# A two-step graph layer with nucleus attention on one core: ACT copies results out of PSUM, the kept weights' sum comes from the mask pass, queries are projected at the head of a slot

## The chip, the cores and the metric

The kernel runs on one NeuronCore of a Trainium2 chip. Its engines are PE (matrix products, into PSUM), DVE (vector operations), ACT (functions of one operand with scale and bias), POOL (a second, slower vector engine, here for columns of one number per row) and SP (which only issues transfers here). Each takes its own instructions in order and waits on semaphores for the others. The metric is the time of one execution on the device in microseconds; less is better.

## The reference

The input x is 3327x256, adj (S) 3327x3327 with few entries off zero. All is float32. The layer does two steps of diffusion and of attention, and a layer norm at the end:

```python
R = S + jnp.eye(N, dtype=X.dtype)
R = R / R.sum(-1, keepdims=True)
Z = jnp.zeros_like(X)
Xf = X
Xa = X
for n in range(STEPS):                               # 2 steps
    A = _top_p_attention(Xa, W1, W2, W3)
    Xf = R @ Xf
    Xa = A @ Xa
    Z = Z + Xf @ U1[n].T + Xa @ U2[n].T
h = X + Z                                            # then (h - mean) / sqrt(var + eps) * g + b
```

and `_top_p_attention` is a softmax of which each row keeps only its largest entries, until their sum reaches 0.9, scaled to sum 1 again:

```python
q = X @ W1.T @ W2.T
k = X @ W3.T
probs = jax.nn.softmax(q @ k.T / TAU, axis=-1)
idx = jnp.argsort(-probs, axis=-1)
sp = jnp.take_along_axis(probs, idx, axis=-1)
cs = jnp.cumsum(sp, axis=-1)
keep_sorted = cs - sp < TOP_P
mask = jnp.zeros(probs.shape, dtype=bool).at[rows, idx].set(keep_sorted)
A = probs * mask
return A / jnp.maximum(A.sum(-1, keepdims=True), 1e-12)
```

The X of this is `h = max(layernorm(x), 0)` of the input x, and the output is x plus what the layer returns.

## The kernel before

Rows are cut into 26 tiles of 128. A step goes through the tiles in slots: the loop at the end of `guess_graph_layer` (L719 to L750) has in slot i four tiles in different stages of work.

- `settle(i)` on DVE decides which weights of tile i are kept. L585 is a pass over the 128x3328 weights `e` that keeps in `w` those under a guessed cut, with their sum; 20 MAX8 (L589) and 5 or 6 rounds (L594, L596) find the largest of what is left; L605, the mask pass, sets to zero in `e` what is not kept. POOL gives the wanted sum (`need`, L586).
- `first(i + 1)` and in step 1 `second(i + 1)` guess the cut of the next tile. `first` makes two passes over `e` on ACT (L520) and then a chain on POOL of one-column operations (L524 to L542). `second` makes one more pass on DVE (`jv`, L549) and a longer POOL chain (L551 to L574). The column that they end with is what L585 waits for.
- `spread(i + 1)` gives the 26 matmuls of diffusion (`diffuse`, L662), which come out of a generator and are put between others; each needs a piece of adj, which SP loads five blocks of 128x128 at a time (`AD`, `at`, three buffers).
- `attend(i - 1)` multiplies the kept weights by Xa: 26 transposes of `e` (`pt`, L637), each four copied out of PSUM by ACT (`eT`, L639), 26 matmuls into `pa` (L647). Column 256 of the right side is 1, so column 256 of `pa` is the sum of the kept weights. DVE takes its reciprocal (L651), ACT scales by it (L652).
- `weights(i + 2)` projects the queries of the tile after (PE, `pq`, L455 and L457; ACT copies `qT`; DVE takes from PSUM what a first guess needs, L462 to L465), makes the logits (PE, `pl`, L476) and their exps (ACT, L480 to L484), and sums and guesses on POOL (L489 to L511).
- Then what is left of diffusion, and in step 0 `prep(1, ...)`, which makes keys and queries of step 1 from the tile, in step 1 `finish`, which multiplies by U1 and U2 (`pz`), adds X (DVE, L684, out of PSUM), norms, adds x and writes the rows out (SP, L693).

A scheduler puts every engine's instructions in one order before the program runs, from the order of the code and its own estimates. What an engine does at a given moment is fixed by that order alone: an instruction whose semaphore has not come holds back all that stand behind it. PSUM holds two buffers each of `pl` and `pt` (which `pq`, `pk` and `pg` share), and one each of `pa` (which `pz` shares) and `pr`.

`search_graph_layer` is another, slower way to the same result, taken only where a guess has failed; it doesn't run in these executions.

## Time and profile before

| | |
|---|---|
| time, median of 3 runs | 2558.28 us (2556.28 to 2563.46) |
| the profiled execution | 2557.2 us |
| its span in the trace | 2555.4 us |
| mean granted clock of PE in it | 0.877 |
| busy: PE, weight load, DVE, ACT, POOL | 1945.5 (76%), 1524.5 (60%), 1100.5 (43%), 866.6 (34%), 900.7 (35%) us |
| moved by DMA | 102.24 MB, 40 GB/s over the span |

The span is the time from the first to the last instruction that the trace shows; 1.8 us of the execution's own time lie around it. Times below count from the span's start. In a row, L585 is line 585 of the kernel; `w<-e,g` are the tiles that it writes and reads. A number in brackets at a row's end is the time in which the engine stood idle before it, with the instruction whose end released it. Two rows that follow each other may overlap by up to 0.2 us, since an instruction begins while the one ahead of it still writes. A row may stand for several equal instructions in succession (x8). PE does a float32 matmul in two passes, which count as two, and a transpose in one.

### The profile page before, as it was taken

Reading aid. Unit: us, or ns where it says so; the run is one execution under the profiler, and the core shown is the slowest. Engines: PE = TensorE matmul, PEld = TensorE weight load, DVE = VectorE, ACT = ScalarE, POOL = GpSimd, SP = SyncE. Lnnn points to the kernel's source line nnn. Section 1 sums busy time; section 2 is a strip of 40 time slices with the busy share of each in tenths; the row PEclk is TensorE's granted clock in tenths of the full one; section 3 lists DMA queues with packets and bytes.
Section 4 is the critical chain, followed back from the end, with each engine's and each line's share of the span. In section 5 each row is a group of like instructions: output and inputs, shape, how many; then the busy total and the mean of one; then the engine's idle time right before and its main releaser. Section 6 shows DMA issues by size and latency. Waiting matters only on the chain.

```text
span 2555.4 us, 26919 instructions
## 1 busy us (share of the span) xinstructions
PE 1945.5 (76%) x9055; PEld 1524.5 (60%) x9055; DVE 1100.5 (43%) x2969; ACT 866.6 (34%) x1588; POOL 900.7 (35%) x2541
## 2 busy tenths in 40 slices
PE   6957887888888887887777767777667776777767
PEld 5735665766666675775556645566455664556645
DVE  2155543535354443531754454344543445434451
ACT  4344344343434334234232223322233222332221
POOL 4153222232322222214534433344333443334431
PEclk9978888999999998988888887888878888888888
DMA  4210011111111111111111111111111111111100
GB/s 133 69 29 27 13 32 43 39 48 33 48 44 39 48 39 43 39 39 31 49 32 45 37 32 37 36 46 38 31 34 39 46 38 31 40 34 45 38 26 12
DMA packets 58597, 102.24 MB, mean 40 GB/s; under 512 B 7250, under 2 KB 25169, under 8 KB 58449
## 3 DMA queue, kind: packets, MB, share of 16 engines
q1 hardware_dynamic: 55936, 98.85, 13.3%
q10 hardware_dynamic: 2512, 1.57, 0.2%
q8 instruction: 73, 1.20, 0.2%
q14 instruction: 76, 0.61, 0.1%
HBM read 96.99 MB, written 3.41 MB: 39 GB/s over the span
## 4 chain that ended last, share of the span: by engine, by line
DVE 33%; POOL 29%; PE 14%; ACT 13%; issue 9%; DMA 0%; ACTq 0%; POOLq 0%; DVEq 0%
DVE cand L589 9%; DVE w L585 7%; ACT ja L520 7%; DVE e L605 7%; PE pl L476 4%; ACT e L480 4%; POOL g L564 4%; DVE cand L596 3%; DVE bb L594 3%; PE pz L681 3%; PE pa L647 2%; PE pr L662 2%; POOL g L503 1%; POOL g L499 1%; POOL g L507 1%
## 5 line engine op out<-in xcount | busy, mean ns | idle before, releaser
L476 PE MATMUL pl<-k,qT 64*128 64x512 f32 (+1 forms) x832 | 226.0, 672 | 357.4 <-ACT e L480 321.8
L639 ACT COPY eT<-pt 128x512 f32<-128x512 f32 (+1 forms) x364 | 197.7, 556 | 706.8 <-PE pt L637 704.1
L520 ACT ACTIVATE ja<-e,g 128x3328 uint8<-128x3328 f32 x104 | 319.3, 3070 | 237.5 <-POOL g L503 237.4
L476 PEld LDWEIGHTS pl<-k,qT 64*128 64x128 f32 x832 | 87.8, 232 | 494.1 <-ACT e L480 400.8
L662 PE MATMUL pr<-xf,at 128*128 128x256 f32 x1352 | 368.9, 409 | 16.8 <-ACT xf L671 15.6
L585 DVE SCALAR_TENSOR_TENSOR w<-e,g 128x3328 f32<-128x3328 f32 x52 | 192.0, 3693 | 438.0 <-POOL g L574 225.2
L662 PE MATMUL pr<-x,at 128*128 128x257 f32 x1352 | 371.7, 417 | 0.3 <-DMA at<-in_adj 0.2
L647 PE MATMUL pa<-x,eT 128*128 128x257 f32 x1352 | 326.6, 386 | 10.6 <-ACT eT L639 10.6
L647 PE MATMUL pa<-xa,eT 128*128 128x257 f32 x1352 | 319.5, 380 | 0.5 <-ACT eT L639 0.5
L662 PEld LDWEIGHTS pr<-x,at 128*128 128x128 f32 x1352 | 267.9, 211 | 46.1 <-issue 4.2
L662 PEld LDWEIGHTS pr<-xf,at 128*128 128x128 f32 x1352 | 253.7, 203 | 59.5 <-ACT xf L671 20.1
L647 PEld LDWEIGHTS pa<-x,eT 128*128 128x128 f32 x1352 | 254.8, 193 | 46.9 <-ACT eT L639 11.9
L647 PEld LDWEIGHTS pa<-xa,eT 128*128 128x128 f32 x1352 | 255.1, 190 | 37.3 <-ACT eT L639 1.2
L589 DVE MAX8 cand<-w 128x8 f32<-128x168 f32 (+1 forms) x1040 | 249.2, 317 | 1.6
L637 PE MATMUL pt<-ident,e 128*128 128x128 f32 x1352 | 227.5, 301 | 4.7 <-DVE e L605 4.7
L637 PEld LDWEIGHTS pt<-ident,e 128*128 128x128 f32 x1352 | 189.0, 157 | 41.3 <-DVE e L605 5.1
L489 POOL TENSOR_SCALAR g<-mq 128x1 f32<-128x1 f32 x52 | 17.8, 342 | 510.0 <-DVE rec L607 335.5
L605 DVE SCALAR_TENSOR_TENSOR e<-e,rec 128x3328 f32<-128x3328 f32 x52 | 191.5, 3682 | 4.6
L681 PE MATMUL pz<-u,xT 128*128 128x256 f32 x416 | 121.7, 444 | 83.8 <-ACT xT L415 83.7
L480 ACT ACTIVATE e<-pl 128x1024 f32<-128x1024 f32 x156 | 158.5, 1021 | 69.7 <-PE pl L476 69.7
L652 ACT ACTIVATE xa<-pa,ra 128x256 f32<-128x256 f32 (+1 forms) x52 | 24.7, 475 | 437.1 <-DVE ra L651 437.1
L681 PEld LDWEIGHTS pz<-u,xT 128*128 128x128 f32 x416 | 89.7, 221 | 109.3 <-ACT xT L415 94.6
(160 smaller groups left out, 2018.9 us busy)
## 6 DMA issues: line engine op xcount, KB each, us to landing
at<-in_adj SPq DMA_DIRECT2D x260, 320.0 KB, 3.0
x<-in_x SPq DMA_DIRECT2D x13, 256.0 KB, 4.1
xr<-in_x SPq DMA_DIRECT2D x26, 128.0 KB, 2.2
at<-in_adj SPq DMA_DIRECT2D x52, 64.0 KB, 1.8
out<-y SPq DMA_DIRECT2D x25, 128.0 KB, 1.7
u<-in_u1t ACTq DMA_DIRECT2D x2, 256.0 KB, 6.6
u<-in_u2t ACTq DMA_DIRECT2D x2, 256.0 KB, 7.5
wk<-in_w3t ACTq DMA_DIRECT2D x2, 64.0 KB, 3.9
```

Source lines behind the costliest of these rows:

```text
L476: PE.matmul(pl[:, a, :wd], qT[p, :], keys[step][p].rearrange("p a b -> p (a b)")[:, c : c + wd], start=True, stop=True)
L480: S.activation(e.rearrange("p (a n) -> p a n", a=2)[:, :, c : c + wd], pl[:, :, :wd], AF.Exp, accum_out=za[:, n : n + 1])
L520: S.activation(ja, e, f, bias=col(9), scale=-1.0, accum_out=oa[:, k : k + 1])
L564: G.tensor_scalar(col(7), c1, col(1), 14.0, ALU.mult, ALU.mult)
L585: V.scalar_tensor_tensor(w, e, col(16), e, ALU.is_lt, ALU.mult, accum_out=d2)
L589: V.max(cand[:, 8 * s : 8 * s + 8], w[:, s * SEG : min(NP, (s + 1) * SEG)])
L605: V.scalar_tensor_tensor(e, e, at(1), e, ALU.is_ge, ALU.mult)
L637: PE.transpose(pt[:, j, :], e[:, (j0 + j) * P : (j0 + j + 1) * P], ident)
L639: S.copy(eT[:, :w, :], pt[:, :w, :])
L647: PE.matmul(pa, eT[:, j, :], xa[:, j0 + j, :], start=j0 + j == 0, stop=j0 + j == NT - 1)
L662: PE.matmul(pr[:, :w], at[:, j, :], xf[:, j0 + j, :w], start=j0 + j == 0, stop=j0 + j == NT - 1)
L681: PE.matmul(pz[:, :D], xT[:, c, :], u[:, n, c, :], start=i == 0 and c == 0, stop=i == 3 and c == ND - 1)
```

## The change

Four things are changed.

- `project`, the first part of `weights`, is a function of its own and stands ahead of `attend` in the slot. The values that POOL's first guess needs are copied out of PSUM by ACT (L463) and go on from SBUF (POOL L466, DVE L467). `weights` also puts a matmul of diffusion between its last logits.
- The mask pass (L613) gives the sum of what it keeps by its accumulator, and DVE inverts it there (L614). `attend` leaves the column of ones out, and its scaled copy (L660) reads that reciprocal.
- Results that DVE took from PSUM are copied by ACT: `gt` for the sums of keys (POOL adds it then), `tm` for the diffused rows of step 0 (DVE adds and scales), `y` in `finish`.
- adj is loaded four blocks at a time instead of five, and the table of how many diffusion matmuls stand between attend's groups is (4, 4, 4, 4, 3, 3, 0).

```diff
--- before.py
+++ after.py
@@ -319,3 +319,3 @@
 HALF = NT // 2
-AD = 5
+AD = 4
 
@@ -435,3 +435,5 @@
         PE.matmul(pg[:DA, 0, : DA + 1], kr[:, :DA], kr, start=True, stop=True)
-        V.tensor_tensor(gsum[:, step, :], gsum[:, step, :], pg[:DA, 0, : DA + 1], ALU.add)
+        gt = small.tile([DA, DA + 1], F32, tag="gt", name="gt", bufs=2)
+        S.copy(gt, pg[:DA, 0, : DA + 1])
+        G.tensor_tensor(gsum[:, step, :], gsum[:, step, :], gt, ALU.add)
 
@@ -450,3 +452,3 @@
 
-    def weights(step, t):
+    def project(step, t):
         h, j = divmod(t, HALF)
@@ -455,13 +457,16 @@
         PE.matmul(pq[:, 0, :], w2d[qp, :], qry[qp, j, :], start=True, stop=True)
-        pr_ = pq[:, 1:3, :].rearrange("p a b -> p (a b)")
-        PE.matmul(pr_[:, : 2 * DA + 2], qry[qp, j, :], qm[qp, step, :], start=True, stop=True)
+        pr_ = pq[:, 1:3, :].rearrange("p a b -> p (a b)")[:, : 2 * DA + 2]
+        PE.matmul(pr_, qry[qp, j, :], qm[qp, step, :], start=True, stop=True)
         qT = tpool.tile([P, P], F32, tag="qT", name="qT", bufs=2)
         S.copy(qT, pq[:, 0, :])
-        mq = small.tile([P, 4], F32, tag="mq", name="mq")
-        qj = small.tile([P, DA], F32, tag="qj", name="qj", bufs=1)
-        V.tensor_copy(mq[:, 0:2], pr_[:, 2 * DA : 2 * DA + 2])
-        qs = small.tile([P, DA], F32, tag="qs", name="qs", bufs=1)
-        V.tensor_copy(qs, pr_[:, :DA])
-        V.scalar_tensor_tensor(qj, qs, 1.0, pr_[:, DA : 2 * DA], ALU.mult, ALU.mult,
-                               accum_out=mq[:, 2:3])
+        mq = small.tile([P, 2 * DA + 2], F32, tag="mq", name="mq", bufs=2)
+        S.copy(mq, pr_)
+
+        ms = small.tile([P, 3], F32, tag="ms", name="ms")
+        G.tensor_copy(ms[:, 0:2], mq[:, 2 * DA :])
+        V.scalar_tensor_tensor(mq[:, :DA], mq[:, :DA], 1.0, mq[:, DA : 2 * DA], ALU.mult, ALU.mult,
+                               accum_out=ms[:, 2:3])
+        return qT, ms
+
+    def weights(step, t, qT, ms, fill):
         e = epool.tile([P, NP], F32, tag="e", name="e")
@@ -471,2 +476,4 @@
         for n, c in enumerate(range(0, w, 512)):
+            if n >= 2:
+                fill()
             wd = min(512, w - c)
@@ -486,3 +493,3 @@
         col = lambda k: g[:, k : k + 1]
-        m, nm, qq, Z = mq[:, 0:1], mq[:, 1:2], mq[:, 2:3], rec[:, step, 3, t : t + 1]
+        m, nm, qq, Z = ms[:, 0:1], ms[:, 1:2], ms[:, 2:3], rec[:, step, 3, t : t + 1]
         y = col(4)
@@ -604,3 +611,5 @@
         V.tensor_reduce(at(1), cum[:, :n], AX.X, ALU.min)
-        V.scalar_tensor_tensor(e, e, at(1), e, ALU.is_ge, ALU.mult)
+        r["ra"] = ra = small.tile([P, 1], F32, tag="ra", name="ra")
+        V.scalar_tensor_tensor(e, e, at(1), e, ALU.is_ge, ALU.mult, accum_out=ra)
+        V.reciprocal(ra, ra)
         V.tensor_tensor(cum[:, :n], dr[:, :n], b, ALU.mult)
@@ -628,4 +637,5 @@
 
-    def attend(e, xa, dst, n, fill):
-        pa = ps_a.tile([P, D + 1], F32, tag="pa", name="pa")
+    def attend(r, xa, dst, n, fill):
+        e = r["e"]
+        pa = ps_a.tile([P, D], F32, tag="pa", name="pa")
         starts = list(range(0, NT, 4))
@@ -646,8 +656,6 @@
             for j in range(min(4, NT - j0)):
-                PE.matmul(pa, eT[:, j, :], xa[:, j0 + j, :],
+                PE.matmul(pa, eT[:, j, :], xa[:, j0 + j, :D],
                           start=j0 + j == 0, stop=j0 + j == NT - 1)
             eT = nxt
-        ra = small.tile([P, 1], F32, tag="ra", name="ra")
-        V.reciprocal(ra, pa[:, D : D + 1])
-        S.activation(dst[:n], pa[:n, :D], AF.Copy, scale=ra[:n])
+        S.activation(dst[:n], pa[:n], AF.Copy, scale=r["ra"][:n])
 
@@ -667,7 +675,11 @@
         if w > D:
-            rs = small.tile([P, 1], F32, tag="rs", name="rs")
-            V.tensor_scalar(rs, pr[:, D : D + 1], 1.0, None, ALU.add)
-            V.reciprocal(rr, rs)
-        S.activation(dst, pr[:, :D], AF.Copy, scale=rr)
-        V.scalar_tensor_tensor(dst, xf[:, t, :D], rr, dst, ALU.mult, ALU.add)
+            tm = row.tile([P, D + 1], F32, tag="xf2", name="tm", bufs=3)
+            S.copy(tm, pr)
+            V.tensor_scalar(rr, tm[:, D : D + 1], 1.0, None, ALU.add)
+            V.reciprocal(rr, rr)
+            V.tensor_tensor(tm[:, :D], tm[:, :D], xf[:, t, :D], ALU.add)
+            V.tensor_scalar(dst, tm[:, :D], rr, None, ALU.mult)
+        else:
+            S.activation(dst, pr[:, :D], AF.Copy, scale=rr)
+            V.scalar_tensor_tensor(dst, xf[:, t, :D], rr, dst, ALU.mult, ALU.add)
 
@@ -676,3 +688,3 @@
         parts = ((xf1[:, t, :], u1, 0), (xa1[:, t, :D], u2, 0), (xf2, u1, 1), (xa2, u2, 1))
-        pz = ps_a.tile([P, D + 1], F32, tag="pa", name="pz")
+        pz = ps_a.tile([P, D], F32, tag="pa", name="pz")
         for i, (rows, u, n) in enumerate(parts):
@@ -680,6 +692,7 @@
             for c in range(ND):
-                PE.matmul(pz[:, :D], xT[:, c, :], u[:, n, c, :],
+                PE.matmul(pz, xT[:, c, :], u[:, n, c, :],
                           start=i == 0 and c == 0, stop=i == 3 and c == ND - 1)
         y = row.tile([P, D], F32, tag="xa2", name="y")
-        V.tensor_tensor(y, pz[:, :D], x0[:, t, :D], ALU.add)
+        S.copy(y, pz)
+        V.tensor_tensor(y, y, x0[:, t, :D], ALU.add)
         xr = row.tile([P, D], F32, tag="xr", name="xr")
@@ -725,5 +738,7 @@
             work = spread(step, i + 1) if 0 <= i + 1 < NT else iter(())
+            if 0 <= i + 2 < NT:
+                qT, ms = project(step, i + 2)
 
             def fill(k):
-                run(work, (4, 4, 4, 4, 4, 3, 0)[k])
+                run(work, (4, 4, 4, 4, 3, 3, 0)[k])
                 if k in (1, 3):
@@ -735,6 +750,6 @@
                 if step == 0:
-                    attend(r["e"], x0, xa1[:, t, :D], rows_of(t), fill)
+                    attend(r, x0, xa1[:, t, :D], rows_of(t), fill)
                 else:
                     xa2 = row.tile([P, D], F32, tag="xa2", name="xa2")
-                    attend(r["e"], xa1, xa2, P, fill)
+                    attend(r, xa1, xa2, P, fill)
             run(meas, 3)
@@ -743,3 +758,3 @@
             if 0 <= i + 2 < NT:
-                live[step, i + 2] = weights(step, i + 2)
+                live[step, i + 2] = weights(step, i + 2, qT, ms, lambda: run(work, 1))
             run(work, NT)
```

The scheduler's order changes with it. On DVE in the middle of step 0, the rows of before from the mask pass (L605) of a tile on; `ra` is the reciprocal for attend, `mq`, `qs` and `qj` are the query's values:

```order
L605 SCALAR_TENSOR_TENSOR e_3462<-e_3462,rec_156 128x3328 [waits DVE_49,Activation_49]
L606 TENSOR_TENSOR cum_3825<-dr_3827,bb_157 128x40
L607 TENSOR_REDUCE rec_156<-cum_3825 128x1 [waits DVE_49]
L651 RECIPROCAL ra_3704<-pa_3578 128x1 [waits PE_49]
L462 COPY mq_3712<-pq_3707 128x2 [waits Activation_49]
L464 COPY qs_3715<-pq_3707 128x64
L465 SCALAR_TENSOR_TENSOR qj_3713,mq_3712<-qs_3715,pq_3707 128x64 [waits DVE_49]
```

and the same place now, on to the next tile's first settle pass (L592); `tm` is the copy of diffused rows:

```order
L613 SCALAR_TENSOR_TENSOR e_3811,ra_4188<-e_3811,rec_156 128x3328 [waits DVE_49,PE_49]
L615 TENSOR_TENSOR cum_4182<-dr_4184,bb_157 128x40
L614 RECIPROCAL ra_4188<-ra_4188 128x1 [waits DVE_49]
L616 TENSOR_REDUCE rec_156<-cum_4182 128x1 [waits DVE_49]
L678 TENSOR_SCALAR rrs_101<-tm_4120 128x1 [waits Activation_49]
L680 TENSOR_TENSOR tm_4120<-tm_4120,x0_95 128x256
L679 RECIPROCAL rrs_101<-rrs_101 128x1 [waits DVE_49]
L681 TENSOR_SCALAR xf1_96<-tm_4120,rrs_101 128x256 [waits DVE_49]
L467 SCALAR_TENSOR_TENSOR mq_4198,ms_4200<-mq_4198 128x64 [waits Activation_49]
L592 SCALAR_TENSOR_TENSOR w_4408,d2_4406<-e_4071,g_4093 128x3328 [waits Pool_49]
```

The reciprocal L651, which read `pa` after PE, stood behind the mask pass; now L614 stands there and reads the mask pass's own sum, and nothing in these rows reads PSUM.

On ACT in the middle of step 0, the end of an attend and the start of the next tile's weights, before:

```order
L639 COPY eT_4203<-pt_4200 128x256 [waits PE_49,Activation_49]
L652 ACTIVATE xa1_97<-pa_4090,ra_4216 128x256 [waits DVE_49]
L459 COPY qT_4222<-pq_4219 128x128 [waits PE_49]
L480 ACTIVATE e_4230,za_4231<-pl_4233 128x2x512 [waits PE_49]
L480 ACTIVATE e_4230,za_4231<-pl_4237 128x2x512 [waits PE_49]
```

and now, from the second 128x3328 pass (`ja`) on; `gt`, `qT` and `mq` are copies out of PSUM:

```order
L527 ACTIVATE ja_4539,oa_4502<-e_4331,g_4353 128x3328 [waits Activation_49]
L437 COPY gt_4403<-pg_4401 64x65 [waits PE_49]
L461 COPY qT_4456<-pq_4453 128x128 [waits PE_49]
L463 COPY mq_4458<-pq_4453 128x130 [waits DVE_49]
L649 COPY eT_4469<-pt_4464 128x512 [waits PE_49]
L649 COPY eT_4476<-pt_4471 128x512 [waits PE_49]
```

The copy of the query `qT` stood behind the scaled copy L652 and ahead of the exps; now it stands with `gt` and `mq` ahead of the first `eT`, seven of which come before the scaled copy, now L660.

On POOL in step 1, from the last operation of the weights' chain (L503) through `first`'s chain (L524 to L530), before; L405, L406, L690 and L691 belong to `finish`:

```order
L503 TENSOR_TENSOR g_10561<-pwr_142,g_10561 128x1 [waits Pool_49]
L405 TENSOR_SCALAR rstd_10625<-mv_10624 128x1 [waits DVE_49]
L406 TENSOR_TENSOR rstd_10625<-rstd_10625,pwr_142 128x1 [waits Pool_49]
L524 TENSOR_SCALAR g_10561<-oa_10722 128x1 [waits Activation_49]
L525 TENSOR_SCALAR g_10561<-g_10561,oa_10722 128x1 [waits Pool_49]
L526 TENSOR_SCALAR g_10561<-g_10561 128x1 [waits Pool_49]
L690 TENSOR_TENSOR y_10618<-y_10618,gam_131 128x256 [waits DMAHW5_49,DVE_49,PE_49]
L528 TENSOR_SCALAR g_10561<-g_10561 128x1 [waits Pool_49]
L554 TENSOR_SCALAR g_10561<-g_10561 128x1
L691 TENSOR_TENSOR y_10618<-y_10618,xr_10620 128x256 [waits Pool_49]
L529 TENSOR_TENSOR g_10561<-g_10561 128x1 [waits Pool_49]
L530 TENSOR_SCALAR g_10561<-g_10561 128x1 [waits Pool_49]
```

and now, from the last operation of `first`'s chain (L537) to the start of `second`'s (L558, which waits for `jv`):

```order
L537 TENSOR_SCALAR g_8926<-g_8926 128x1 [waits Pool_49]
L466 COPY ms_9056<-mq_9054 128x2 [waits Activation_49]
L571 TENSOR_SCALAR g_8926<-g_8926 128x1 [waits Pool_49]
L496 TENSOR_SCALAR g_9228<-ms_9056 128x1 [waits DVE_49,Pool_49]
L497 TENSOR_TENSOR g_9228<-g_9228,pwr_142 128x1 [waits Pool_49]
L498 TENSOR_SCALAR g_9228<-g_9228,ms_9056 128x1
L500 TENSOR_TENSOR g_9228<-g_9228,ms_9056 128x1
L499 TENSOR_TENSOR g_9228<-pwr_142,g_9228 128x1 [waits Pool_49]
L558 TENSOR_SCALAR g_8926<-d1_9181,g_8926 128x1 [waits DVE_49]
L405 TENSOR_SCALAR rstd_8990<-mv_8989 128x1 [waits DVE_49]
L560 TENSOR_SCALAR g_8926<-g_8926 128x1 [waits Pool_49]
L579 TENSOR_SCALAR g_8926<-g_8926 128x1
```

Ahead of `second`'s chain there are now the next tile's first weights operations (L496 to L500), and `finish`'s operations stand among and behind it.

On SP in step 1, transfers around the output's, before:

```order
L660 DMA at_11617<-in_adj 128x640 [waits DMAHW7_49,PE_49]
L660 DMA at_11638<-in_adj 128x640 [waits DMAHW0_49,PE_49]
L660 DMA at_11656<-in_adj 128x640 [waits DMAHW1_49,PE_49]
L693 DMA out_0<-y_11518 128x256 [waits DMAHW5_49,Pool_49]
L686 DMA xr_11820<-in_x 128x256 [waits DMAHW6_49]
L660 DMA at_11691<-in_adj 128x640 [waits DMAHW2_49,PE_49]
```

and now:

```order
L668 DMA at_11811<-in_adj 128x512 [waits DMAHW7_49,PE_49]
L668 DMA at_11831<-in_adj 128x512 [waits DMAHW0_49,PE_49]
L668 DMA at_11848<-in_adj 128x512 [waits DMAHW1_49,PE_49]
L668 DMA at_11873<-in_adj 128x512 [waits DMAHW5_49,DMAHW2_49,PE_49]
L706 DMA out_0<-y_11700 128x256 [waits DMAHW6_49,Pool_49]
L699 DMA xr_12005<-in_x 128x256
```

One adj transfer more stands ahead of the output's, and each is of four blocks.

## Rows read from the trace of the kernel before

**Rows 1.** Page part 5: the last two columns: busy, mean ns | idle before, releaser.
```profile
L652 ACT ACTIVATE xa<-pa,ra 128x256 f32<-128x256 f32 (+1 forms) x52 | 24.7, 475 | 437.1 <-DVE ra L651 437.1
```

**Rows 2.** L585 from 410 to 1110: count, ns min/median/max, first and last start.
```profile
L585 DVE SCALAR_TENSOR_TENSOR w<-e,g x18: 3683/3684/3686, 411.1 to 1108.8; 128x3328 f32<-128x3328 f32 x18
```

**Rows 3.** L585 from 1304 to 2477, same columns.
```profile
L585 DVE SCALAR_TENSOR_TENSOR w<-e,g x23: 3683/3685/4122, 1304.3 to 2475.8; 128x3328 f32<-128x3328 f32 x23
```

**Rows 4.** Table by stage: window, its length, busy us (instructions), clock, DMA, GB/s.
```profile
780.75:821.35 40.60, 34.78 (x172) 27.73 (x171) 18.23 (x52) 16.24 (x29) 11.39 (x38) 0.96 0.14 43
1879.00:1932.00 53.00, 37.91 (x184) 30.01 (x183) 23.74 (x59) 15.83 (x28) 21.82 (x57) 0.87 0.13 40
1932.00:1985.00 53.00, 37.83 (x169) 29.92 (x168) 22.90 (x58) 16.20 (x28) 21.11 (x55) 0.81 0.12 36
```

**Rows 5.** Timeline of DVE, a slot of step 0: start, length, instruction.
```profile
794.03 3.68 DVE L605 SCALAR_TENSOR_TENSOR e<-e,rec 128x3328 f32<-128x3328 f32 x1
...
821.35 3.68 DVE L585 SCALAR_TENSOR_TENSOR w<-e,g 128x3328 f32<-128x3328 f32 x1 [7.57 <-POOL g L542]
```

**Rows 6.** Timeline of PE, the same slot.
```profile
795.76 0.81 PE L647 MATMUL pa<-x,eT 128*128 128x257 f32 x3
...
813.46 1.97 PE L637 MATMUL pt<-ident,e 128*128 128x128 f32 x8
```

**Rows 7.** Timeline of ACT, the same slot.
```profile
798.16 0.47 ACT L652 ACTIVATE xa<-pa,ra 128x256 f32<-128x256 f32 x1 [5.04 <-DVE ra L651]
798.54 0.26 ACT L459 COPY qT<-pq 128x128 f32<-128x128 f32 x1
...
803.63 0.28 ACT L484 ACTIVATE e<-pl 128x127 f32<-128x127 f32 x1
...
809.16 3.07 ACT L520 ACTIVATE ja<-e,g 128x3328 uint8<-128x3328 f32 x1 [4.40 <-POOL g L503]
...
812.88 3.07 ACT L520 ACTIVATE ja<-e,g 128x3328 uint8<-128x3328 f32 x1
```

**Rows 8.** Timeline of PE, a slot of step 1.
```profile
1893.15 2.77 PE L647 MATMUL pa<-xa,eT 128*128 128x257 f32 x12
```

**Rows 9.** Timeline of ACT, the same slot.
```profile
1909.52 0.47 ACT L652 ACTIVATE xa<-pa,ra 128x256 f32<-128x256 f32 x1 [12.65 <-DVE ra L651]
...
1914.44 0.28 ACT L484 ACTIVATE e<-pl 128x127 f32<-128x127 f32 x1
...
1923.34 3.08 ACT L520 ACTIVATE ja<-e,g 128x3328 uint8<-128x3328 f32 x1
```

**Rows 10.** Timeline of DVE, the same slot.
```profile
1879.11 3.69 DVE L549 SCALAR_TENSOR_TENSOR jv<-e,g 128x3328 f32<-128x3328 f32 x1 [3.79 <-POOL g L530]
...
1891.58 3.68 DVE L585 SCALAR_TENSOR_TENSOR w<-e,g 128x3328 f32<-128x3328 f32 x1 [8.78 <-POOL g L574]
...
1905.68 3.68 DVE L605 SCALAR_TENSOR_TENSOR e<-e,rec 128x3328 f32<-128x3328 f32 x1
```

**Rows 11.** Timeline of POOL, the same slot.
```profile
1879.17 3.75 POOL L564 TENSOR_SCALAR g<-g 128x1 f32<-128x1 f32 x1
1883.00 0.72 POOL L687 TENSOR_TENSOR xr<-xr,bet 128x256 f32<-128x256 f32 x1
...
1910.00 0.34 POOL L489 TENSOR_SCALAR g<-mq 128x1 f32<-128x1 f32 x1 [14.19 <-DVE rec L607]
...
1911.33 0.54 POOL L492 TENSOR_TENSOR g<-pwr,g 128x1 f32<-128x1 f32 x1
...
1919.15 0.57 POOL L503 TENSOR_TENSOR g<-pwr,g 128x1 f32<-128x1 f32 x1
```

**Rows 12.** Timeline of ACT, an early slot of step 0.
```profile
239.38 0.48 ACT L652 ACTIVATE xa<-pa,ra 128x256 f32<-128x256 f32 x1 [2.33 <-DVE ra L651]
...
242.00 0.29 ACT L484 ACTIVATE e<-pl 128x127 f32<-128x127 f32 x1
```

**Rows 13.** Page part 6: DMA issues, KB each, us from issue to landing.
```profile
at<-in_adj SPq DMA_DIRECT2D x260, 320.0 KB, 3.0
```

## Prediction

> **What bounds the kernel now.** I read the costliest groups first, for what stands idle and on whom. The scaled copy that ends an attend (L652 on ACT) waits 437.1 us for the reciprocal L651 on DVE, once per tile [rows 1]. Next, the starts of L585, the first pass of a tile's settle, give the slot: in step 0, 18 starts from 411.1 to 1108.8, so 697.7 / 17 = 41.04 us [rows 2]; in step 1, 23 starts from 1304.3 to 2475.8, so 1171.5 / 22 = 53.25 us [rows 3]. The table by stage then shows that no engine fills a slot: PE is busy 34.78 of 40.60 us in a slot of step 0 and 37.91 of 53.00 in one of step 1, DVE 18.23 and 23.74, POOL 11.39 and 21.82 [rows 4]. So it is a loop of waits, and the timelines show it.
>
> Step 0, in the slot that begins at 780.75 [rows 4]: settle's mask pass L605 ends at 797.71, L651 stands right behind it, and L652 starts at 798.16 although attend's last matmul was done at 795.76 + 0.81 = 796.57 [rows 5 to 7]. Behind L652 stand the query copy, the exps (until 803.91), POOL's short chain (until 809.1), the two 128x3328 passes L520 (until 815.95), POOL's first chain, and the next L585 at 821.35. That closes the loop. Step 1 is the same with more of it: PE had finished at 1893.15 + 2.77 = 1895.92 [rows 8], L652 started at 1909.52 after 12.65 us of idle [rows 9], and settle had started only at 1891.58 since the second chain with jv (L549) stands ahead of it [rows 10, 11].
>
> **The change part by part.** Below T0 is the end of the second L520 pass of a slot, where ACT is free again. Times are against the profiled execution, 2557.2 us, which is 1.1 us under the median of the runs.
>
> The kept sum in the mask pass: L605 gets an accumulator. L585 and L549 are the same pass with one and take 3.68 to 3.69, as does L605 without [rows 5, 10], so this costs nothing but a DVE read-out; the reciprocal moves with it, to a tile whose attend comes a slot later. L652 then waits for PE alone. What is late next is attend itself, so the slot becomes the PE and ACT chain.
>
> Queries projected early: qT and the 128x130 copy are made at T0, ahead of the eT copies. What that is worth is in the trace: in an early slot, where the query was ready, the exps ended 242.29 - 239.38 = 2.91 us after L652 began; in the slot of step 0 it was 803.91 - 798.16 = 5.75 [rows 7, 12]. The price is two or three small ACT copies at T0 (0.26 each [rows 7]), about 0.75 us in step 0 and 0.9 in step 1 where y's copy is among them; the transposes behind them wait for these PSUM buffers.
>
> New step 0 slot. Before, T0 was 815.95 - 40.6 = 775.35, so attend ended 796.57 - 775.35 = 21.2 after it. Of this, seven matmuls of diffuse go out (8 in the new attend, 15 before); one costs two passes of 2.77 / 12 = 0.23 [rows 8], so -3.2. Added are 0.75 for the copies and 1.0 for four to eight transposes that used to be done before T0 (eight took 1.97 [rows 6]). Attend: 19.7. Logits and exps, with two diffuse matmuls between: 803.91 - 798.54 = 5.4 [rows 7], so 25.1. POOL chain 5.2, so 30.3; both L520 passes with copies between them 6.8 [rows 7], so the next T0 at 37.1. Gain 41.04 - 37.1 = 3.9, times 17 slots: 67 us. Settle fits: POOL's first chain 5.3 (815.95 to 821.35) plus 2.1 of new POOL work (the next tile's first five weights ops, 1910.00 to 1911.87 [rows 11], and a small copy), so settle runs from 7.5 and its mask pass from 20.8 to 24.5, beside attend.
>
> New step 1 slot. Before, T0 was 1926.42 - 53.25 = 1873.2, and attend ended 22.7 after it. Copies +0.9, transposes +0.5, one diffuse matmul less -0.46: 23.6. Exps: 29.0. POOL chain (1914.72 to 1919.72 [rows 9, 11]) 5.0: 34.0. Both L520 passes (1919.72 to 1926.42) 6.7: next T0 at 40.8, if nothing else interferes. Settle: before it began 1891.58 - 1873.2 = 18.4 after T0. Now 2.1 of the next tile's ops stand ahead of it on POOL, and the xr addition (0.72 [rows 11]) moves behind it. That gives 19.8; as some of the added ops fill gaps between dependent ones, I take 19.4 (between 18.8 and 20.0). Its mask pass starts 1905.68 - 1891.58 = 14.1 later [rows 10]: 33.5 to 37.2.
>
> That is the new question. POOL's chain ends at 34.0, and a POOL operation that starts beside such a DVE pass is held to the pass's end: L564, a 128x1 operation, starts at 1879.17, beside L549 from 1879.11 to 1882.80, and takes 3.75 us [rows 10, 11]. The Trainium skill ("SBUF — State Buffer", Who interferes with whom) says why: the pair of SBUF ports that both use is an exclusive lock for a whole instruction. The trace agrees with 3.75 against some 0.3 for its neighbours; by that rule alone, every collision costs what is left of the pass and none a fraction.
>
> If the mask pass begins before POOL's last operation (0.57 [rows 11]) has started, the chain ends near 37.7 and the slot is 44.4; if not, it is 40.8. The border lies at a mask pass start of 34.0 - 0.57 = 33.4, which is my estimate itself. What tips it is attend's end, and that moves by more than the margin: of two neighbouring slots one had a granted clock of 0.87, the next 0.81 [rows 4], and 7% of 23 us is 1.6 us. A slower attend pushes the chain into the pass, a faster one out of it. So I take half the slots: mean 42.6, gain 10.6 x 22 = 234 us.
>
> The rest. ACT copies pr (128x257) and DVE adds and scales out of SBUF: off the loop, since those end during the POOL chain; bounds 0 and one copy of 0.5 per slot of step 0 (8 us). gsum and y by way of ACT: 0.2 to 0.5 us at T0, in the sum. AD 4 instead of 5: one more transfer a tile, 320 KB landed in 3.0 us at the median [rows 13] and three buffers hold 12 tiles instead of 15; nothing waited on it, so 0, at worst 0.3 us x 39 slots = 12 us, at best -5. Start, boundary between the steps and end: no slots with the loop; 0, bounds -10 and +10.
>
> Sum: 2557.2 - 67 - 234 = 2256, and against the median 2257. I say 2258.
>
> **The rivals.** (a) No slot of step 1 collides: 2557 - 67 - 22 x 12.45 = 2216. For it: the slow stretches after PE's idle time (eight transposes in 1.97 us [rows 6], where twelve longer passes of attend took 2.77 [rows 8]) may shrink as PE waits less. Against it: every added link in the loop brings its own delay.
>
> (b) All of them collide: 2557 - 67 - 22 x 8.85 = 2295. For it: attend estimated 0.5 too short is enough. If in step 0, too, the mask pass (20.8 to 24.5) is met by the chain's start (25.1, only 0.6 behind it), 17 x 3.7 = 63 us go: 2358. The Trainium skill ("Perfetto Trace Analysis", Optimizing Scalar/DVE Operations) warns that work moved between GPSIMD and DVE may gain nothing because of the shared port. The rows show this port held in one place of a slot; by the warning this case would be the one to expect, at 2295 to 2358.
>
> (c) Slower: SP's queue. In step 1 the output transfer (out<-y) waits for the last y op on POOL, which now stands behind jv and the next tile's ops, and adj transfers needed near the end of attend are queued behind it. I put that y op at T0 + 15.4 (4 us ahead of settle's start); an adj transfer lands 3.0 later [rows 13], at 18.4, and is needed at about 20. From 1.6 us of delay on, each us lengthens attend by one. To turn the total round it must eat (67 + 234) / 22 = 13.7 us a slot, so y would have to come after T0 + 30.7. Then the kernel would take 2557 or more, 2600 at T0 + 32.7. For it: POOL is in order and frozen by each pass. Against it: only one pass, jv's, lies ahead of y.
>
> (d) The loop isn't what I think, and another wait takes the place at once, as POOL's and DVE's own loop: settle start to settle start in step 1 through jv, second chain and settle is 19.4 + 17.8 = 37.2 after T0, so it does not bind. PE can't fall below its 34.8 and 37.9 us a slot, which at 37.1 and 40.8 would be 94 and 93% busy; should it bind at a lower clock (0.81 against 0.87), slots of 40 and 44 remain: 2340.
>
> **How the numbers follow.** Some slots collide (2235 to 2280): 0.40. (a), 2190 to 2235: 0.20. (b) and a PE that binds, 2280 to 2400: 0.30. Little comes of it: 0.04. (c): 0.06. Range 2195 to 2370, which leaves out the tail of (b), (c) and a little below. About 0.3% is what a measurement here can tell from no change; faster 0.91, the same 0.03, slower 0.06.
>
> **What would show it.** In the profile after, L660 must wait for PE, no longer for DVE; the slots must be near 37 and between 40.8 and 44.4; POOL's chain ahead of L527 must show an operation of up to 3.7 us in the slots that collide and none in the others; the granted clock in such slots should be the lower. Wrong it is if step 0 keeps 41 us, if L660 or the eT copies wait for something new, if diffuse's matmuls wait for adj behind out<-y, or if a collision shows in every slot or in none.

## The result, and the profile after

The changed kernel takes 2204.4 us (median of 4 runs, 2193.6 to 2213.0) against 2559.0, a ratio of 0.861 with an interval of 0.856 to 0.866. The forecast was 2258 with a range of 2195 to 2370. Here and below, an execution more than 1.5% above the fastest of its kernel is left out of medians and ratios. The profiled execution took 2195.93 us, its span is 2194.1, and the mean granted clock went from 0.877 to 0.936.

The group that waited for DVE before [rows 1], in the same columns:

```profile
L660 ACT ACTIVATE xa<-pa,ra 128x256 f32<-128x256 f32 (+1 forms) x52 | 24.7, 475 | 174.0 <-PE pa L657 124.1 <-DVE dr L609 24.0 <-POOL need L593 17.6
```

Most of its waiting (124.1 of 174.0 us) is now for attend's last matmul. The starts of settle's first pass (L592), which answer to [rows 2] and [rows 3]:

```profile
L592 DVE SCALAR_TENSOR_TENSOR w<-e,g x18: 3683/3684/3686, 400.2 to 1039.2; 128x3328 f32<-128x3328 f32 x18
...
L592 DVE SCALAR_TENSOR_TENSOR w<-e,g x23: 3684/4123/4128, 1231.1 to 2126.3; 128x3328 f32<-128x3328 f32 x23
```

A slot of step 0 lasts 639.0 / 17 = 37.59 us (41.04 before), one of step 1 895.3 / 22 = 40.70 (53.25). The 361.3 us between the two spans are 10.9 at the start, 58.6 in step 0, 3.7 at the boundary, 276.2 in step 1 and 11.8 at the end.

The table by stage (columns as in [rows 4], the busy times in the order PE, weight load, DVE, ACT, POOL): a slot of step 0, a usual and a long slot of step 1, and then the first six us of attend in a long and in a usual slot.

```profile
619.83:657.45 37.62, 33.65 (x163) 26.14 (x162) 17.83 (x51) 15.97 (x32) 11.95 (x40) 0.95 0.17 47
1420.27:1460.33 40.06, 36.58 (x177) 28.25 (x176) 23.46 (x57) 16.73 (x32) 21.55 (x56) 0.97 0.18 50
1374.84:1420.27 45.43, 38.22 (x174) 29.99 (x173) 23.44 (x57) 16.62 (x31) 25.30 (x56) 0.88 0.16 44
1374.00:1380.00 6.00, 6.00 (x22) 4.59 (x21) 3.13 (x5) 2.32 (x7) 4.41 (x9) 0.55 0.00 0
1420.50:1426.50 6.00, 6.00 (x35) 5.21 (x35) 4.21 (x5) 2.57 (x6) 5.43 (x9) 1.00 0.01 3
```

Step 1 has two kinds of slot: 17 of 38.6 to 40.4 us and four of 45.1 to 45.4; the first, of 36.5, stands apart. What parts them stands on POOL, in the chain between the exps and the next tile's passes. First the long slot, then the usual one (timeline: start, length, instruction):

```profile
1404.72 0.20 POOL L501 TENSOR_TENSOR g<-za 128x2 f32<-128x2 f32 x1 [6.54 <-ACT e L490]
...
1408.07 3.76 POOL L508 TENSOR_SCALAR g<-g 128x1 f32<-128x1 f32 x1
...
1413.01 0.57 POOL L510 TENSOR_TENSOR g<-pwr,g 128x1 f32<-128x1 f32 x1
...
1448.49 0.20 POOL L501 TENSOR_TENSOR g<-za 128x2 f32<-128x2 f32 x1 [4.91 <-ACT e L490]
...
1451.85 0.26 POOL L508 TENSOR_SCALAR g<-g 128x1 f32<-128x1 f32 x1
...
1453.07 0.57 POOL L510 TENSOR_TENSOR g<-pwr,g 128x1 f32<-128x1 f32 x1
```

and DVE's mask pass in the same two slots:

```profile
1407.97 3.69 DVE L613 SCALAR_TENSOR_TENSOR e<-e,rec 128x3328 f32<-128x3328 f32 x1
...
1453.40 3.69 DVE L613 SCALAR_TENSOR_TENSOR e<-e,rec 128x3328 f32<-128x3328 f32 x1
```

The same one-column operation L508 takes 0.26, or 3.76 when it starts 0.10 behind the mask pass; it ends 0.17 after the pass. In the usual slot the chain's last operation L510 starts 0.33 ahead of the pass. The chain is late in the long slot because attend was slow, and PE's timeline (in brackets the idle time before, and on what) shows why:

```profile
1371.64 2.91 PE L693 MATMUL pz<-u,xT 128*128 128x256 f32 x8 [3.36 <-ACT xT L415]
...
1376.56 2.76 PE L670 MATMUL pr<-xf,at 128*128 128x256 f32 x6
...
1417.08 3.59 PE L693 MATMUL pz<-u,xT 128*128 128x256 f32 x8 [7.08 <-ACT xT L415]
...
1421.74 1.46 PE L670 MATMUL pr<-xf,at 128*128 128x256 f32 x6
```

In both slots PE pauses for `xT`, which stands behind the first `ja` pass on ACT. Then the same six matmuls take 2.76 us at 0.55 of the clock, or 1.46 at 1.00. The slow start follows the shorter of the two pauses. Both in the table by stage:

```profile
1368.28:1371.64 3.36, 0.01 (x1) 0.00 (x0) 3.36 (x3) 3.36 (x4) 0.00 (x0) 1.00 0.28 78
1410.00:1417.08 7.08, 0.00 (x1) 0.00 (x1) 2.41 (x6) 3.47 (x4) 3.48 (x5) 0.75 0.13 38
```

In the longer pause the clock fell while PE still stood idle, so the products `pz` behind it took 3.59 us, and attend began at 1.00. In the shorter one it stood at 1.00 to the end and fell behind it, on attend's start. The longer pause is itself the work of a held chain, and in this execution no long slot follows another. So attend ends 24.7 us after T0 instead of 23.1, the exps follow, and the chain runs into the mask pass.

### The profile page after: what moved, and what is told of

Read it like the earlier page. It is cut to its first block, busy times and chain, and to the rows that moved or that the text cites. A ratio compares the mean times of both kernels' runs of the same rounds, so it can differ in the third digit from the quotient of the medians.

```text
span 2194.1 us, 27211 instructions
## 1 busy us (share of the span) xinstructions
PE 1889.8 (86%) x9055; PEld 1464.7 (67%) x9055; DVE 1085.7 (49%) x2891; ACT 894.8 (41%) x1718; POOL 960.0 (44%) x2645
## 3 DMA queue, kind: packets, MB, share of 16 engines
q10 hardware_dynamic: 2512, 1.57, 0.3%
## 4 chain that ended last, share of the span: by engine, by line
PE 64%; POOL 18%; issue 9%; ACT 7%; DMA 2%; DVE 1%; SPq 0%; POOLq 0%; ACTq 0%; DVEq 0%
PE pa L657 25%; PE pr L670 19%; PE pl L483 7%; PE pt L647 6%; PE pz L693 4%; ACT e L487 3%; ACT ja L527 2%; POOL g L514 1%; POOL g L506 1%; POOL g L510 1%; DMA at<-in_adj 1%; POOL g L571 1%; POOL g L508 1%; PE pq L457 1%; POOL g L502 1%
## 5 line engine op out<-in xcount | busy, mean ns | idle before, releaser
L670 PE MATMUL pr<-x,at 128*128 128x257 f32 x1352 | 391.3, 427 | 6.2 <-ACT tm L677 4.4
L592 DVE SCALAR_TENSOR_TENSOR w<-e,g 128x3328 f32<-128x3328 f32 x52 | 200.8, 3862 | 388.8 <-POOL g L581 197.7
L657 PE MATMUL pa<-x,eT 128*128 128x256 f32 x1352 | 322.7, 383 | 9.4 <-ACT eT L649 9.4
L657 PE MATMUL pa<-xa,eT 128*128 128x256 f32 x1352 | 318.3, 379 | 0.5 <-ACT eT L649 0.5
L670 PEld LDWEIGHTS pr<-xf,at 128*128 128x128 f32 x1352 | 240.4, 194 | 96.0 <-issue 38.6
L483 PE MATMUL pl<-k,qT 64*128 64x512 f32 (+1 forms) x832 | 200.5, 568 | 46.9 <-ACT e L487 46.9
L647 PE MATMUL pt<-ident,e 128*128 128x128 f32 x1352 | 208.5, 278 | 2.1 <-ACT gt L437 1.5
L647 PEld LDWEIGHTS pt<-ident,e 128*128 128x128 f32 x1352 | 169.8, 143 | 42.4 <-issue 4.9
L613 DVE SCALAR_TENSOR_TENSOR e<-e,rec 128x3328 f32<-128x3328 f32 x52 | 191.6, 3684 | 3.4
L483 PEld LDWEIGHTS pl<-k,qT 64*128 64x128 f32 x832 | 70.3, 190 | 129.6 <-ACT e L487 72.8
L501 POOL TENSOR_TENSOR g<-za 128x2 f32<-128x2 f32 x52 | 13.4, 259 | 298.3 <-ACT e L490 298.1
L467 DVE SCALAR_TENSOR_TENSOR mq<-mq 128x64 f32<-128x64 f32 x52 | 12.2, 236 | 248.1 <-ACT mq L463 248.1
```

The costliest lines, as they stand in the source:

```text
L483: PE.matmul(pl[:, a, :wd], qT[p, :], keys[step][p].rearrange("p a b -> p (a b)")[:, c : c + wd], start=True, stop=True)
L592: V.scalar_tensor_tensor(w, e, col(16), e, ALU.is_lt, ALU.mult, accum_out=d2)
L613: V.scalar_tensor_tensor(e, e, at(1), e, ALU.is_ge, ALU.mult, accum_out=ra)
L647: PE.transpose(pt[:, j, :], e[:, (j0 + j) * P : (j0 + j + 1) * P], ident)
L657: PE.matmul(pa, eT[:, j, :], xa[:, j0 + j, :D], start=j0 + j == 0, stop=j0 + j == NT - 1)
L670: PE.matmul(pr[:, :w], at[:, j, :], xf[:, j0 + j, :w], start=j0 + j == 0, stop=j0 + j == NT - 1)
```

## The experiments

Each is compared with the kernel before in the same series. The first four undo or isolate a part. **The changed kernel, with the kept sum from attend's column again:**

```diff
-        V.scalar_tensor_tensor(e, e, at(1), e, ALU.is_ge, ALU.mult, accum_out=ra)
+        V.scalar_tensor_tensor(e, e, at(1), e, ALU.is_ge, ALU.mult)
...
-        S.activation(dst[:n], pa[:n], AF.Copy, scale=r["ra"][:n])
+        V.reciprocal(ra, pa[:, D : D + 1])
+        S.activation(dst[:n], pa[:n, :D], AF.Copy, scale=ra[:n])
```

> The changed kernel with one part undone: the kept sum again comes from column 256 of pa, and DVE inverts it behind the mask pass. Theory A (two things stood behind the mask pass on DVE, the kept sum's reciprocal and the query's values, and either alone holds the loop): in step 0 settle runs from 7.5 us after the second ja pass, its mask pass ends at 24.5, the scaled copy comes at 24.7 instead of 20.2 and the exps end at 27.6 instead of 25.4: slots of 39.8 us instead of 37.6. In step 1 the mask pass ends at 36.9, the exps at 40, the slot takes 51.9 instead of 40.7. Sum 2204 + 17 x 2.2 + 22 x 11.2 = 2490 us. Theory B (the early projection carries most of the gain, the sum little): the slots stay within 1.5 us of the changed kernel's, 2200 to 2265 us.

Measured: 2548.6 us, ratio 0.9966 (0.9951 to 0.9982). The reciprocal stands behind the mask pass again (DVE, step 1):

```profile
1603.93 3.69 DVE L612 SCALAR_TENSOR_TENSOR e<-e,rec 128x3328 f32<-128x3328 f32 x1
1607.54 0.16 DVE L659 RECIPROCAL ra<-pa 128x1 f32<-128x1 f32 x1
```

L660 starts at 1607.78, though attend's last matmul was done at 1595.64. The slot is 51.4 in step 1, near the 51.9 expected, and 42.4 in step 0, where 39.8 was expected and the kernel before takes 41.0: the last logits wait for the scaled copy too and then run at a lower clock. So the time misses the 2490 expected. The other parts together, without this one, are worth 9 us.

**The changed kernel, with the projection called behind attend again:**

```diff
-            if 0 <= i + 2 < NT:
-                qT, ms = project(step, i + 2)
...
             if 0 <= i + 2 < NT:
+                qT, ms = project(step, i + 2)
```

> The changed kernel with one part undone: the projection of the queries stands again with the weights, behind attend. Theory A: in step 0 the exps end about 0.6 us later and POOL's first five weights operations, which need the query's values, run right ahead of the chain: 38.9 us a slot instead of 37.6. In step 1 DVE's product for them (L467) stands behind the mask pass, which ends at 34.8; POOL's five operations and the chain follow, until 42, and the slot takes 48.9 instead of 40.7. Sum 2204 + 17 x 1.3 + 22 x 8.2 = 2406 us. Theory B (early projection saves only its own two matmuls and one copy, about 1 us a slot): 2204 + 39 x 1 = 2243 us.

Measured: 2385.3 us, ratio 0.9323 (0.9303 to 0.9343); slots of 38.0 and 48.8. In step 1 DVE's sum over the query's values (L467) stands behind the mask pass:

```profile
1500.35 3.69 DVE L613 SCALAR_TENSOR_TENSOR e<-e,rec 128x3328 f32<-128x3328 f32 x1
1503.96 0.22 DVE L467 SCALAR_TENSOR_TENSOR mq<-mq 128x64 f32<-128x64 f32 x1
```

POOL's chain begins with it, at 1504.37, while the last exp had ended at 1498.78. So the query's values held the loop too, not only the reciprocal.

**The changed kernel, with DVE reading PSUM again** (key sums, query values, diffused rows, `y`), in part:

```diff
-            S.copy(tm, pr)
-            V.tensor_scalar(rr, tm[:, D : D + 1], 1.0, None, ALU.add)
+            V.tensor_scalar(rs, pr[:, D : D + 1], 1.0, None, ALU.add)
...
-        S.copy(y, pz)
-        V.tensor_tensor(y, y, x0[:, t, :D], ALU.add)
+        V.tensor_tensor(y, pz, x0[:, t, :D], ALU.add)
```

> The changed kernel with one part undone: DVE reads the key sums, the query's values, the diffused rows of step 0 and finish's rows out of PSUM again, ACT copies only the query. Theory A: these stood beside other work, and ACT gets back 0.4 to 0.6 us at the head of a slot, on the path; in step 1 DVE's order puts y's operations ahead of jv, so settle and its mask pass come up to 1 us later, which makes a meeting with POOL's chain rarer: 2165 to 2225 us. Theory B (DVE, which takes its instructions in order, is held by waiting for PE's results in PSUM): over 2270 us.

Measured: 2223.3 us (2208 to 2241), ratio 0.8692 (0.8632 to 0.8751). That is inside the first range, but not for its reason. The trace is of an execution of 2242.9 us: there step 1 alternates between 39 and 46 us (42.3 in the mean), so meetings are more frequent, not rarer, though the mask pass comes 0.9 us later or more. ACT's copies are worth some 20 us by the ratios, give or take as much. That this comes by way of the same meeting is shown for that execution alone.

**The kernel before, with the kept sum from the mask pass alone:**

```diff
-        V.scalar_tensor_tensor(e, e, at(1), e, ALU.is_ge, ALU.mult)
+        V.scalar_tensor_tensor(e, e, at(1), e, ALU.is_ge, ALU.mult, accum_out=ra)
+        V.reciprocal(ra, ra)
```

> The kernel before with one part of the change alone: the mask pass gives the kept sum. Theory A: the query's values still stand behind the mask pass on DVE, so in step 1 POOL's chain cannot start before 38.5 us after the second ja pass, and the slot takes 50.2 instead of 53.25; in step 0 it takes 39.7 instead of 41.04: 2559 - 22 x 3 - 17 x 1.3 = 2470 us. Theory C (the scaled copy's wait of 437 us was the loop, and freeing it alone brings what it brought together with the rest): 2260 to 2350 us.

Measured: 2457.1 us, ratio 0.9604 (0.9583 to 0.9625); slots of 38.5 and 51.2. The sum alone gives 101 us, all without it 9, together they give 355. By slots, in step 0 the sum alone gives 2.6 of 3.5 us, so there it was the loop. In step 1 the sum alone gives 2.1 of 12.6, all without it 1.9, and all without the early projection 4.5: two results stood behind one pass, and either alone keeps most of the loop.

Loading adj by four blocks, the new table and the diffusion matmuls between the logits were not tested by themselves.

The next four test the meeting. **Five operations (times 1) on POOL ahead of settle in step 1**, so that its mask pass comes later:

```diff
+        for _ in range(5):
+            G.tensor_scalar(col(16), col(16), 1.0, None, ALU.mult)
```

> The changed kernel with five more one-column operations at the end of step 1's second POOL chain (each multiplies by 1), ahead of settle: its first pass and its mask pass start about 2.0 us later, at 20.7 and 35.2 us after the second ja pass. Theory A (in the long slots of 45.4 us, POOL's chain meets the mask pass and is held for 3.7 us; they are the slots in which attend ends at 24.7, after a start at the lower clock): the chain now ends ahead of the mask pass even there, no operation of it takes over 0.6 us, the slots are 39.2 to 41.8, the time falls by 18 us or more and the spread between runs shrinks: 2165 to 2185 us. Theory B (these slots are long because of attend's slow start and what follows from it, the meeting costs nothing of its own): as the changed kernel, 2194 to 2213 us, or slower by the five operations.

Measured: 2197.1 us (2192 to 2198), ratio 0.8606 (0.8584 to 0.8629). The mask pass starts at 34.6, and chains that start at 29.9 are no longer held: they end at 35.0 (38.7 before), and these slots take 41.7 (45.4). One slot near the head of step 1, whose attend ended only at 26.0, was still held: L511 took 3.68 us beside the pass, and the slot 46.8. And eight of 22 slots now have the slow attend (24.7 and more), where four of 22 had it, so the mean slot is 40.6 as before. The hold is confirmed, and the forecast of the time missed: slow starts took back what the hold gave. Why they became more frequent was not tested.

**The next tile's first five POOL operations behind settle's, in step 1**, so that the mask pass comes earlier:

```diff
+        else:
+            with tc.issue_after(last.ins):
+                early()
```

> The changed kernel, but in step 1 the next tile's first five POOL weights operations are issued behind the second chain, not ahead of it: settle and its mask pass come about 1.9 us earlier, the mask pass from 31.2 to 34.9 us after the second ja pass. Theory A: POOL's chain, from 28.2 on, meets it in every slot; what is left of it runs from 34.9, so the slot is 43.8 and up to 45.5 after a slow start, on average 44.0 instead of 40.7: 2204 + 22 x 3.3 = 2275 us. Theory B (settle is off the path now, so its place costs nothing): 2190 to 2215 us.

Measured: 2275.0 us, ratio 0.8917 (0.8891 to 0.8943). The mask pass starts at 30.4, and every slot but the first is held (43.1 to 45.9). One of them, on POOL and then on DVE:

```profile
1420.72 3.55 POOL L511 TENSOR_SCALAR g<-g 128x1 f32<-128x1 f32 x1
```

```profile
1420.50 3.69 DVE L619 SCALAR_TENSOR_TENSOR e<-e,rec 128x3328 f32<-128x3328 f32 x1
```

**Diffusion matmuls moved out of attend into PE's pause** (11 in step 0, 7 in step 1):

```diff
+            def mid():
+                run(ahead, (13, 9)[step])
```

> The changed kernel with diffusion matmuls of the next slot moved ahead: 11 instead of 7 stand in step 0, and 7 instead of 3 in step 1, where PE waits for ACT's copies between the two ja passes, and 3 fewer in attend. Theory A (PE's pause there costs twice, by its length and by the lower clock with which attend begins): attend ends at 18.1 in step 0 and at 21.3 in step 1 instead of 20.2 and 23.1; in step 0 the chain then meets the mask pass (20.8 to 24.5) and ends at 29.8, slots 36.5 instead of 37.6; in step 1 38.4 instead of 40.7 with no meeting: 2204 - 22 x 1.1 - 22 x 2.3 = 2130 us. Theory B (PE is near its bound and the moved matmuls delay finish's products and the next query as much as they spare attend): 2190 to 2215 us.

Measured: 2261.5 us, ratio 0.8863 (0.8838 to 0.8889). Both expectations fell. Attend ends at 20.2 and 23.5 where it ended at 20.2 and 23.1, since its start stayed slow, and the mask pass came 0.6 earlier, so every slot of step 1 but the first is held (44.37).

**The same, and step 0's five POOL operations behind its first chain:**

```diff
+        r["last"] = G.tensor_tensor(col(16), col(5), col(8), ALU.add)
```

> As the kernel with diffusion matmuls moved ahead, and in step 0 the next tile's first five POOL weights operations behind the first chain, so that settle and its mask pass come 1.9 us earlier there: 18.9 to 22.6 us. Theory A: in step 0 POOL's chain, from 23.3 on, comes after the mask pass and is not held: slots of 35.4 instead of 36.5: 2130 - 22 x 1.1 = 2106 us. Theory B (meetings in step 0 cost nothing): as that kernel, within 8 us.

Measured: 2258.1 us, ratio 0.8861 (0.8831 to 0.8891), as the second expectation said. Some early slots of step 0 last 35.4 us (attend 18.1), those from 576 us on 37.5 (20.2). PE in one of each:

```profile
501.57 0.30 PE L436 MATMUL pg<-kr 128*64 128x65 f32 x2 [2.52 <-issue]
...
502.44 1.57 PE L677 MATMUL pr<-x,at 128*128 128x257 f32 x6
...
723.13 0.45 PE L436 MATMUL pg<-kr 128*64 128x65 f32 x2 [2.53 <-issue]
...
724.67 2.94 PE L677 MATMUL pr<-x,at 128*128 128x257 f32 x6
```

and the table by stage around them:

```profile
502.44:508.44 6.00, 5.33 (x30) 4.34 (x30) 0.27 (x2) 3.59 (x7) 3.10 (x11) 1.00 0.10 25
...
723.00:729.00 6.00, 5.87 (x20) 4.88 (x21) 0.27 (x2) 4.02 (x7) 2.40 (x10) 0.50 0.04 12
```

The same work after the same pause of 2.5 us: once the clock stays at 2.4 GHz, once it is at 1.2. That is 2.1 us of the slot, and it can't be read off the pause's length.

The last three work on the pauses. **The pause split and shortened** (14 diffusion matmuls ahead of the key sums in step 0; in step 1 the first `ja` ordered behind the copy that PE waits for):

```diff
+                with tc.issue_after(hold["xT"].ins):
+                    S.activation(ja, e, f, bias=col(9), scale=-1.0, accum_out=oa[:, k : k + 1])
```

> The changed kernel with PE's pause ahead of attend filled by work that has to be done anyway: in step 0, 14 diffusion matmuls of the next slot (instead of 7) stand between the projections and the key sums, and the next tile's first five POOL operations behind the first chain; in step 1 the last two transposed copies are issued ahead of the first ja pass on ACT, so that finish's products end early, and 7 matmuls and the next query follow them. Theory A (what is left to gain is that pause: its length, the low clock of the 6 us behind it, and through both the meetings of POOL's chain with the mask pass): attend ends at 16.6 in step 0 and 21.2 in step 1, the first passes of an attend run at full clock in nearly every slot, slots of 34.7 and 38.2 us: 2204 - 22 x 2.9 - 22 x 2.5 = 2085 us, between 2065 and 2110. Theory B (the clock falls for a reason that a filled pause does not touch, as in the kernels with 11 and 7 matmuls moved): the low clock stays, slots of 37.5 and 40 to 44: 2190 to 2260 us.

Measured: 2179.5 us, ratio 0.8510 (0.8499 to 0.8522), between the two expectations. Step 0 keeps 37.6; a clock of 0.50 follows two pauses of 1.2 and 2.2 us as well, which lie 0.9 us apart. Step 1 is 39.7 in every slot, without a hold.

**The same, with products that nothing reads in what was left of the pauses:**

```diff
+        if t >= 3:
+            for _ in range((8, 14)[step]):
+                PE.matmul(pq[:, 3, :], ident, ident, start=True, stop=True)
```

> The kernel with the pause partly filled, and in what is left of it products of the identity with itself that nobody reads: 5 and 8 of them around the key sums in step 0, 14 behind the next query in step 1 (about 0.24 us each at the full clock). No other instruction moves. Theory A (the low clock at an attend's start comes from PE's pause ahead of it): PE is busy through the pause, the clock stays at 1.00, attend ends at 17.9 in step 0 instead of 20.4 and at about 20 in step 1, slots of 35.3 and 38.5 us: 2179 - 22 x 2.3 - 22 x 1.2 = 2102 us, between 2085 and 2130. Theory B (the clock falls for another reason, and work in the pause only delays the next query's copies): 2179 to 2230 us.

Measured: 2173.6 us, ratio 0.8487 (0.8472 to 0.8503), between the two expectations. A slot of each step:

```profile
642.62:677.94 35.32, 34.91 (x189) 27.96 (x188) 17.71 (x51) 15.87 (x32) 14.97 (x40) 1.00 0.18 49
1408.39:1448.05 39.66, 38.12 (x202) 30.58 (x202) 23.02 (x58) 16.36 (x32) 21.52 (x56) 1.00 0.18 51
```

Step 0 does what was expected: clock 1.00, attend 18.0, slot 35.3. That is 2.2 us a slot under the kernel without these products, 38 us in 17 slots, and only 6 arrive in the total. Most of the rest is lost at the start. Five of the products stand in `prep`, which runs there for each of the 26 tiles, where PE has no pause to fill. PE up to 170 us, columns as in [rows 1]; the 130 products count as 260 passes, and this mean holds passes that overlap:

```profile
L432 PE MATMUL pk<-ident 128*128 128x128 f32 x260 | 36.7, 291 | 0.0
```

The regular slots of step 0 begin at 436.1 us instead of 405.9. Step 1 keeps 39.66 although its exps now end at 25.5 after T0, since POOL stands elsewhere:

```profile
1412.32 0.24 POOL L405 TENSOR_SCALAR rstd<-mv 128x1 f32<-128x1 f32 x1 [10.36 <-DVE mv L404]
...
1436.19 0.27 POOL L611 TENSOR_SCALAR need<-rec,d 128x1 f32<-128x1 f32 x1 [3.84 <-DVE w L610]
1436.52 0.10 POOL L482 MEMSET e<- 128x1 f32 x1
1436.57 0.20 POOL L515 TENSOR_TENSOR g<-za 128x2 f32<-128x2 f32 x1
```

The `rstd` of the output rows waits for DVE and delays the first chain, thereby settle (24.0 after T0 instead of 18.7), thereby `need`, behind which the weights' chain is queued. The kernel without the products had this order already.

**The same, with the second half of `finish` behind the next slot's first chain:**

```diff
+            if todo:
+                close(*todo.pop(), live[step, i + 1]["c13"] if 0 <= i + 1 < NT else None)
```

> As the kernel with PE kept busy, and in step 1 the second half of finish (y's sum, norm and output) is written behind the first POOL chain of the next slot, not ahead of it. In that kernel settle starts at 24.0 us after the second ja pass in step 1, since POOL's first chain stands behind y's rstd, which waits for DVE, and POOL's next weights chain, behind settle's wanted sum, starts at 28.2 though the exps have ended at 25.5. Theory A: settle starts at 19 to 20, the chain at 25.5, the mask pass comes after the chain's end, slots of 37.0 instead of 39.7: 2173 - 22 x 2.7 = 2115 us. Theory B (POOL's and DVE's work in step 1 binds whatever its order): 2165 to 2180 us.

Measured: 2138.5 us (2137.5 to 2140.5), ratio 0.8365 (0.8349 to 0.8381), between the expectations and the fastest version: 3% under the changed kernel. A slot of step 1:

```profile
1444.87:1482.77 37.90, 37.90 (x205) 30.66 (x204) 23.47 (x58) 16.56 (x31) 21.14 (x56) 1.00 0.19 53
```

Settle is back at 19.1, the chain ends at 31.5, ahead of the mask pass at 33.1. PE is busy for 37.90 of 37.90 us, 3.4 of them with the unread products, and ACT's first copy of the slot waits for the last of these:

```profile
1445.70 0.27 ACT L469 COPY qT<-pq 128x128 f32<-128x128 f32 x1 [0.74 <-PE pq L467]
```

So PE's work, the unread part included, now stands on the path. Fewer of these products were not tried, neither here nor at the start, whose 30 us this kernel still carries: it would take some 2108 us without them, an estimate from the 436.1 and 405.9 above.

## Why the prediction was right, and where not

The mechanism holds. The accumulator costs next to nothing (L613 takes 3.69, L605 took 3.68), L660 waits for PE, and the slots are near what was worked out. Times after T0, forecast and then measured:

| | attend | exps | chain | settle | mask pass | slot |
|---|---|---|---|---|---|---|
| step 0 | 19.7, 20.2 | 25.1, 25.4 | 30.3, 30.8 | 7.5, 7.5 | 20.8, 20.8 | 37.1, 37.6 |
| step 1, not held | 23.6, 23.1 | 29.0, 28.3 | 34.0, 33.4 | 19.4, 18.7 | 33.5, 33.2 | 40.8, 40.1 |

The difference of 0.5 in step 0 fits one term, the matmuls at attend's start, which the sum took at normal speed (0.23 a pass, 2.8 for twelve). They take 4.56 us behind a pause of 3.72:

```profile
616.96 0.30 PE L435 MATMUL pg<-kr 128*64 128x65 f32 x2 [3.72 <-issue]
...
617.83 4.56 PE L670 MATMUL pr<-x,at 128*128 128x257 f32 x12
```

That is 1.8 us, more than the difference, so other terms of the sum must have been too long by some 1.3; which ones was not tested. What the slow start costs is shown by the experiment with products in the pauses: attend ends at 18.0, and at 19.7 to 20.6 in the kernel that differs by these products alone.

**The step that failed is "So I take half the slots: mean 42.6".** Four of 22 meet, and the mean is 40.7. That is 22 x 1.9 = 42 us of the 60 between the forecast for the profiled execution (2256) and 2196. With four slots at its own prices the forecast would have had a mean of 41.5, so the share is 25 of these us; the others come from slots shorter than the 40.8 of the sum. The place was right, and the two experiments that move the mask pass (to 30.4: all held but the first; to 34.6: one) show it. The trace agrees with the rule of the Trainium skill that the forecast named ("SBUF — State Buffer", Who interferes with whom: the shared ports are held for a whole instruction): 3.76 us beside the pass, 0.26 without it. The forecast could not have told the share: it put the margin at 0, and the chain's last operation in fact starts 0.33 us ahead of the pass. The price was off as well: a met slot costs 5.3, as 1.6 of it is the slow attend that causes the meeting. "A slower attend pushes the chain into the pass" was thus right, and the granted clock of the long slot is the lower, as was forecast.

**The second is "Start, boundary between the steps and end: no slots with the loop; 0, bounds -10 and +10."** They gave 26 us; what shortened each of them was not tested. Step 0 gave 8 us less than the 67 in the sum. Together -42 - 26 + 8 = -60. So the time came out in the range of rival (a), no slot colliding, though not by (a): a few slots do. One of the four executions (2193.6) lies just below the range that was stated.

**What the prediction did not see** is how the gain divides. It gave the loop to the reciprocal L651 alone and priced the early projection by the exps that follow sooner. The experiments show that the query's values, behind the same mask pass, hold POOL's chain in step 1 nearly as firmly: the early projection is worth 181 us once the sum is moved, and the sum 344 once the projection is early, but the sum alone 101. The trace of before had a sign of it. L489 waits 14.19 us for DVE [rows 11], and the chain behind it then waits little for the exps:

```profile
1914.63 0.19 POOL L494 TENSOR_TENSOR g<-za 128x2 f32<-128x2 f32 x1 [2.76 <-ACT e L483]
```

By these rows a slot could gain no more than these 2.76 us from earlier exps, with the query's values where they were; the sum alone gave 2.1. The total was right because the new slot was put together from its own chain, not from gains part by part.

The reading of [rows 12] doesn't price the early projection. In that slot not only the query was ready: ACT had done the first exps 3.45 us ahead of L652. In the changed kernel the exps end 5.2 us after L660 begins; the sum had taken 5.4.

Rival (c), the output transfer in SP's queue, did not show: no slot but the held ones is longer than the sum. Of (d) nothing shows in the changed kernel: PE is busy 36.6 of 40.1 us. Only in the last experiment is PE busy for the whole slot.

## What to carry to other kernels

When a long pass on an in-order engine ends a loop of waits, list everything that is queued behind it: two results there can each hold most of the loop, and moving one gains little (in step 1 here, 2 of 12.6 us). Work out the new period from the new chain. Then ask which operation of another engine stands within a few tenths of a us of a long pass: there a small change of clock decides whether a whole pass is added, and freeing time on one engine can move it into the meeting, as moving matmuls into the pause did here (2261 in place of 2204).
